# A deformable convolution, attention and mixture-of-experts kernel: the preparation of the next image held to a steady pace, and two products issued in 512 columns

## The chip, the cores and the metric

The kernel runs on one core of a Trainium2 chip. The time is the device time of one execution in microseconds. The kernel before took 7870.18 us (median of 3 runs, 7869.32 to 7878.19). The engines named below are PE (TensorE, matrix products), ACT (ScalarE, exponentials), DVE (VectorE), POOL (GpSimd, which here issues the gathers), SP (SyncE, which here issues nearly all other transfers) and the 16 DMA engines.

## The reference

The input is `x` of 4 images, 128 channels, 64 by 64 positions. Layer 0 adds to `x` a deformable 3x3 convolution of its group norm. Layer 1 takes the 4096 positions of an image as tokens of 128 channels: attention with 16 heads of 8 channels in which query, key and value are one and the same tensor, a small feed-forward part, and then 8 experts of which the two best are mixed for each token.

```python
# layer 0
x = x + deform_conv(group_norm(x), offsets and masks from two 3x3 convolutions)
# layer 1, per image: t is 4096 x 128
qkv = ring(cos(heads(ln(t)) + rx_theta))
scores = einsum("bhsd,bhtd->bhst", q, q) / sqrt(8)
ctx = einsum("bhst,bhtd->bhsd", softmax(scores), q)
t = t + ln(x1 + ffn(x1)),  x1 = ln(ln(t) + ctx @ w_comb.T)
t = t + sum over the top 2 of 8 experts of p_k * (ln(t) @ expert_w[k])
```

## The kernel before

**The attention loop.** For each image there are 4 groups of 4 heads, 8 chunks of 512 queries, and key tiles of 128. A *run* is one group and one chunk of queries over its key tiles; a *step* is one key tile of a run. There are 3700 steps, 964 in image 0 and 912 in each of the others. In a step PE makes scores for 4 heads (`scores`, L1155, four products into two PSUM tiles `sc` of 1024 columns), ACT takes their exponential (L1164, two instructions into SBUF tiles `e`), and PE multiplies them with the values (`context`, L1172, four products into `acc`). Scores are issued two steps ahead of the products that use them (`LAG = 2`, L1308); the `sc` tiles have 3 buffers, the `e` tiles 6.

**Turned tiles.** Scores are symmetric, so of two neighbouring chunks one block of 512 by 512 is computed once. `turn` (L1040) transposes the two `e` tiles of such a step on DVE into a tile with tag `st` (3 buffers), SP writes it to DRAM (`etd<-st`), and a later run reads it back (`et<-etd`) and uses it in `from_turned` (L1096, products at L1108).

**Work beside the loop.** Two kinds of work fill the rest of PE, DVE, POOL and the queues. `prepare(b)` makes the keys, queries and values of image b: group norm, a table of corners in DRAM, offsets, and then `deform` (L563), which goes through 96 *units* of three taps and 128 positions: a gather by POOL two units ahead (L575), three weighted sums on DVE (L589 to L592), three transposes into a tile that also has tag `st` (L599), and after each fourth unit a write to DRAM (`smd<-tr`, L612). Each of the 8 chunks of an image then goes through `convolved` (L633: read back as `sT`, L643, then the convolution as products of 256 columns) and `features` (L701). `finish(b, ch)` (L989) is the part behind attention: output projection, feed-forward and experts (L882, 16 products of 256 columns times four column blocks of 32).

**Who sets the order.** The order on PE, DVE, SP and POOL is fixed when the program is built, by the planner `Beside` (L62). It advances an estimated time by 1.82 us a step. Each piece of side work is a generator that yields `need(pe, dve, lat, hold)` before its next piece. In each step the planner takes at most one piece with PE work, and that only if it has credit: 0.44 us of PE a step are granted (`RATE`), at most 0.44 is saved up and 0.50 may be owed (`LATE`, L143); while the first image is streamed in, 1.0 us a step are granted. Among pieces that are ready the lowest rank goes first: turned products -1, `prepare` 0.5 or 2, `finish` 1 or 2. `prepare(b+1)` has rank 2 while its `progress` (L584) is ahead of `share`, the part of image b's steps that is done (counted to 80 steps before its end, L1333), and 0.5 while it is behind (L1334). Whatever of it is left at the last run of image b is drained (L1356). A piece with `hold=True` keeps the one PSUM bank for side work (`misc`) until its group is complete. The order on ACT, and which buffer of a pool a tile gets, is decided by the framework as the program is built.

**By columns.** `by_columns` (L270) makes a product of 128 output rows as four products of 32 rows, one on each column block of the array. An f32 product shows as two records in the profile, so one call shows as eight.

Of the kernel before, what the change touches and what calls it, by code (L numbers as in the profile page):

```python
# [22 lines left out]
P = 128  # L23
# [7 lines left out]
KK = 9  # L31
# [162 lines left out]
FREE = -1.0  # L194


def need(pe=0.0, dve=0.0, lat=0.0, hold=False, after=0.0):

    return pe, dve, lat, hold, after


def ve(n, ops=1):

    return ops * (0.17 + n / 960.0)


MM256 = 0.44
MM128 = 0.23  # L210

# [7 lines left out]
def kernel(  # L219
# [37 lines left out]
    prepared = {}  # L257

    progress = {}
    featuring = []  # L260


# [54 lines left out]
    wconv_sb = load(wconv, [P, KK, C], "wconv_sb")  # L317
# [245 lines left out]
    def deform(b, tab, idx, wt):  # L563


        AHEAD = NV - 1
        units = [
            (ch, kg, j) for ch in range(NCH) for kg in range(3) for j in range(4 * ch, 4 * ch + 4)
        ]

        def gather(_, kg, j):
            v = work.tile([P, 3, 4 * C], F32, tag="v", name=f"v{b}_{j}_{kg}", bufs=NV)
            for k in range(3):
                kk = 3 * kg + k
                nc.gpsimd.indirect_dma_start(  # L575
                    out=v[:, k, :], out_offset=None, in_=tab,
                    in_offset=bass.IndirectOffsetOnAxis(ap=idx[:, j, kk : kk + 1], axis=0),
                )
            return v, beside.gathered()

        sent = 0.0
        ahead = [gather(*units[n]) for n in range(AHEAD)]
        for n, (ch, kg, j) in enumerate(units):
            progress[b] = 0.1 + 0.9 * n / len(units)  # L584
            v, landed = ahead.pop(0)
            v4 = v.rearrange("p k (q c) -> p (k q) c", c=C)
            w12 = wt[:, j, 3 * kg : 3 * kg + 3, :].rearrange("p k q -> p (k q)")
            yield need(dve=ve(1536), after=landed)
            nc.vector.tensor_tensor(v4, v4, w12[:, :, None].to_broadcast([P, 12, C]), ALU.mult)  # L589
            yield need(dve=ve(768) + ve(384))  # L590
            nc.vector.tensor_tensor(v[:, :, : 2 * C], v[:, :, : 2 * C], v[:, :, 2 * C :], ALU.add)  # L591
            nc.vector.tensor_tensor(v[:, :, :C], v[:, :, :C], v[:, :, C : 2 * C], ALU.add)  # L592

            yield need(dve=ve(384))
            if j % 4 == 0:
                beside.flush(sent)
                tr9 = work.tile([P, 4, 4, 4, 32], F32, tag="st", name=f"tr{b}_{ch}_{kg}", bufs=NST)
            for k in range(3):
                nc.vector.transpose(  # L599
                    out=tr9[:, k, :, j % 4, :],  # L600
                    in_=v[:, k, :C].rearrange("p (c i) -> p c i", i=32),
                )
            if n + AHEAD < len(units):
                beside.later(beside.dve, lambda u=units[n + AHEAD]: ahead.append(gather(*u)))
            if j % 4 < 3:
                continue
            while kg == 0 and len(featuring) > 1:
                yield need(lat=1.0)

            def put(ch=ch, kg=kg, tr9=tr9):  # L610
                for o in range(4):
                    nc.sync.dma_start(  # L612
                        out=smd[ch % 2][:, 3 * kg : 3 * kg + 3, :, o].rearrange(
                            "i k c n -> i (k c) n"
                        ),
                        in_=tr9[32 * o : 32 * (o + 1), :3].rearrange("p k c j t -> p (k c) (j t)"),
                    )

            sent = beside.dve
            beside.later(sent, put)  # L620
            if kg == 2:

                while featuring:
                    yield need(lat=1.0)
                featuring.append(True)
                beside.later(
                    beside.dve + 0.1,
                    lambda ch=ch: beside.add("prepare", convolved(b, ch), 0.5, True),
                )
        while featuring:  # L630
            yield need(lat=1.0)

    def convolved(b, ch):  # L633

        xr = work.tile([P, CH], F32, tag="p2", name=f"xr{b}_{ch}", bufs=NP2)
        nc.sync.dma_start(out=xr, in_=xf[b, :, CH * ch : CH * (ch + 1)])
        yield need(lat=2.5)

        sT = big.tile([P, KK, CH], F32, tag="xs", name=f"sT{b}_{ch}")

        def get(kg):
            for c in range(4):
                nc.sync.dma_start(  # L643
                    out=sT[32 * c : 32 * (c + 1), 3 * kg : 3 * kg + 3],
                    in_=smd[ch % 2][:, 3 * kg : 3 * kg + 3, c].rearrange("i k o n -> i k (o n)"),
                )

        get(0)
        yield need(lat=6.0)
        get(1)  # L650
        yield need(lat=4.0)
        for k in range(KK):
            if k == 2:
                get(2)
            for hf in range(2):
                last = k == KK - 1 and hf == 1
                yield need(pe=MM256, dve=ve(128, 4) if last else 0.0, lat=0.2 if last else FREE, hold=not last)
                if k == 0 and hf == 0:
                    po = misc(f"conv_ps{b}_{ch}")
                by_columns(  # L660
                    po[:, 256 * hf : 256 * (hf + 1)], wconv_sb[:, k, :],
                    sT[:, k, 256 * hf : 256 * (hf + 1)], k == 0 and hf == 0, last,
                )
        for o in range(4):
            of_block = xr.rearrange("p (j o t) -> p j o t", o=4, t=32)[:, :, o]
            nc.vector.scalar_tensor_tensor(
                of_block, po[:, P * o : P * (o + 1)].rearrange("p (j t) -> p j t", t=32), bconv_sb,
                of_block, ALU.add, ALU.add,
            )
        yield need(pe=tr(4), dve=ve(512))  # L670
        pt = misc(f"x2_ps{b}_{ch}")
        for k in range(4):
            nc.tensor.transpose(pt[:, P * k : P * (k + 1)], xr[:, P * k : P * (k + 1)], ident)
        x2 = work.tile([P, 4, C], F32, tag="p2", name=f"x2_{b}_{ch}", bufs=NP2)
        nc.vector.tensor_copy(x2, pt.rearrange("p (i c) -> p i c", c=C))
        beside.later(beside.dve, lambda: nc.sync.dma_start(out=x2d[b][ch], in_=x2))
        mean = work.tile([P, 4], F32, tag="lt_m", name=f"mean{b}_{ch}")
        rstd = work.tile([P, 4], F32, tag="lt_r", name=f"rstd{b}_{ch}")
        yield from features(b, ch, x2, mean, rstd)
# [202 lines left out]
    def experts(b, ch, x4):  # L882
# [75 lines left out]
        for i in range(4):  # L958
            ws = [temp2(f"eo{b}_{ch}_{i}_{hf}") for hf in range(2)]
            for hf in range(2):  # L960
                for part in range(2):
                    yield need(pe=MM256, dve=ve(512) if part else 0.0, lat=FREE, hold=not part)
                    if part == 0:
                        pe = misc(f"e_ps{b}_{ch}_{i}_{hf}")
                    e0 = 4 * hf + 2 * part
                    by_columns(
                        pe[:, 256 * part : 256 * (part + 1)], uT[:, P * i : P * (i + 1)],
                        ew_sb[:, e0 : e0 + 2, :].rearrange("p e c -> p (e c)"), True, True,
                    )
                nc.vector.tensor_tensor(  # L970
                    ws[hf], pe.rearrange("p (e c) -> p e c", c=C),
                    gt[:, i, 4 * hf : 4 * (hf + 1), None].to_broadcast([P, 4, C]), ALU.mult,
                )
            yield need(dve=ve(512))
            w = ws[0]
            nc.vector.tensor_tensor(w, w, ws[1], ALU.add)
            yield need(dve=ve(256) + ve(128, 2), lat=0.2)
            nc.vector.tensor_tensor(w[:, :2, :], w[:, :2, :], w[:, 2:4, :], ALU.add)
            nc.vector.tensor_tensor(w[:, 0, :], w[:, 0, :], w[:, 1, :], ALU.add)
            nc.vector.tensor_tensor(x4[:, i, :], x4[:, i, :], w[:, 0, :], ALU.add)  # L980
# [319 lines left out]
    with tc.manual_schedule(engines={PE, DVE, SP, POOL}):  # L1300
# [6 lines left out]
        while n < len(steps):  # L1307
# [23 lines left out]
            if b + 1 < NB:  # L1331

                share = (n - begun) / (of_batch[b] - 80 - begun)  # L1333
                beside.rank("prepare", 2 if progress.get(b + 1, 0.0) > share else 0.5)  # L1334
            beside.step(backlog)
            if issued <= n + LAG and issued < len(steps) and at_hand(issued, n):
                continue
# [15 lines left out]
                beside.drain("turned")  # L1353
            if following:
                if following[0] != b and at == 0:
                    beside.drain("prepare")  # L1356

                if at == 1:
# [97 lines left out]
```

## Time and profile before

| what | us |
|---|---|
| median of 3 runs | 7870.18 |
| the profiled execution | 7908.98 |
| its span | 7907.1 |
| ACT busy, share of the span | 6874.6 (87%) |
| PE busy, share of the span | 7194.3 (91%) |
| DVE busy | 4487.9 (57%) |
| POOL busy | 1644.6 (21%) |
| mean granted TensorE clock | 0.954 |

The profiled execution took 7908.98 us, 0.5% more than the median. The span runs from the first to the last instruction. Times of records of PE overlap, since matmuls are pipelined: where the spacing of instructions matters it is read from their starts in the timeline. In the page, the line of a group gives its busy time, the mean of one, and the engine's idle time before it with what ended most of it. Image 0 is attended from 246 us on, image 1 from 2403 us, image 2 from 4249 us and image 3 from 6122 us; the last exponential of a step starts near 7821 us. POOL's slices show when `deform` runs.

### The profile page before, as it was taken

What the parts mean: (1) busy time and instruction counts of PE and PEld (TensorE: products, weight loads), DVE (VectorE), ACT (ScalarE), POOL (GpSimd) and SP (SyncE); (2) the same over time, 40 slices, a digit from 0 to 9 for tenths busy, and PEclk for the clock granted to TensorE, in tenths of its full rate; (3) what the DMA queues carried; (4) which work ended last, traced back from release to release, by engine and by line L of the source; (5) the groups of instructions that cost most, each with busy time, mean ns of one, the idle gap of its engine ahead of it and who ended that gap; (6) DMA issues with size and microseconds to landing.
All of it is one profiled execution on the core that took longest, in us unless ns stands there. A gap on an engine that the chain in (4) does not pass through costs nothing.

```text
span 7907.1 us, 182019 instructions
## 1 busy us (share of the span) xinstructions
PE 7194.3 (91%) x73664; PEld 2524.1 (32%) x73664; DVE 4487.9 (57%) x9024; ACT 6874.6 (87%) x7441; POOL 1644.6 (21%) x1326
## 2 busy tenths in 40 slices
PE   2378979999998999999999989989999999999997
PEld 1122222333333333333333333333333333333333
DVE  5666436666453667777554567766444554445434
ACT  0267978988998988989999988888999999999995
POOL 4544114343100332332000133432000000000000
PEclk6688988999999999999999999999999999999998
DMA  6776558888666878898666788988655577877762
GB/s 180 215 214 208 158 150 251 272 260 269 194 190 181 254 228 254 261 293 266 189 187 180 211 278 270 286 282 276 188 175 168 157 234 238 256 240 247 241 212 81
DMA packets 968439, 1757.98 MB, mean 222 GB/s; under 512 B 170864, under 2 KB 436088, under 8 KB 916908
## 3 DMA queue, kind: packets, MB, share of 16 engines
q1 hardware_dynamic: 862590, 1436.61, 60.1%
q0 software_dynamic: 92160, 302.06, 11.9%
q8 instruction: 578, 9.47, 0.5%
q10 hardware_dynamic: 12846, 7.67, 0.4%
q14 instruction: 265, 2.17, 0.1%
HBM read 1063.83 MB, written 682.13 MB: 221 GB/s over the span
## 4 chain that ended last, share of the span: by engine, by line
PE 78%; DMA 8%; DVE 3%; SPq 3%; issue 3%; ACT 3%; POOL 1%; another core or an unknown queue 0%; ACTq 0%; DVEq 0%; POOLq 0%
PE acc L1172 38%; PE sc L1155 23%; PE acc L1108 5%; PE e_ps L273 3%; PE conv_ps L273 3%; ACT e L1164 3%; PE f_ps L273 2%; DMA sT<-smd 2%; DMA et<-etd 1%; DMA kT<-kTd 1%; DMA etd<-st 1%; SPq L476 1%; PE om_ps L507 1%; DMA v<-tab,idx 1%; DVE v L589 1%
## 5 line engine op out<-in xcount | busy, mean ns | idle before, releaser
L1164 ACT ACTIVATE e<-sc 128x1024 f32<-128x1024 f32 x7400 | 6871.5, 1065 | 863.7 <-PE sc L1155 584.6
L1172 PE MATMUL acc<-e,qf 128*32 128x512 f32 x29600 | 3982.3, 608 | 46.1 <-DVE cu L1376 32.9
L1155 PE MATMUL sc<-qT,kT 32*128 32x512 f32 x14800 | 2404.0, 502 | 317.8 <-ACT e L1164 148.2
L1155 PEld LDWEIGHTS sc<-qT,kT 32*128 32x128 f32 x14800 | 960.2, 184 | 3745.1 <-ACT e L1164 3089.6
L575 POOL DMA_INDIRECT v<-tab,idx x1152 | 1444.7, 1254 | 1880.2 <-DVE tr L599 1158.3
L1046 DVE STREAM_TRANSPOSE st<-e 128x1024 f32<-128x1024 f32 x792 | 937.8, 1222 | 833.1 <-ACT e L1164 640.7
L1172 PEld LDWEIGHTS acc<-e,qf 128*32 128x32 f32 x29600 | 804.0, 110 | 614.4 <-issue 339.8
L375 POOL TENSOR_TENSOR r<-ln_t,expo 128x4 f32<-128x4 f32 x96 | 112.3, 1170 | 3151.2 <-DVE ln_t L373 3113.4
L589 DVE TENSOR_TENSOR v<-v,wt 128x1536 f32<-128x1536 f32 x384 | 665.9, 1734 | 103.6 <-DMA v<-tab,idx 78.5
L1108 PE MATMUL acc<-et,qf 128*32 128x128 f32 x12672 | 528.7, 283 | 55.5 <-DMA et<-etd 47.5
L273 PE MATMUL conv_ps<-sT,wconv_sb 128*32 128x256 f32 x4608 | 380.7, 407 | 125.0 <-DMA sT<-smd 121.9
L970 DVE TENSOR_TENSOR eo<-e_ps,gt 128x512 f32<-128x512 f32 x256 | 175.0, 685 | 548.7 <-PE e_ps L273 538.3
L1108 PEld LDWEIGHTS acc<-et,qf 128*32 128x32 f32 x12672 | 305.7, 110 | 259.3 <-issue 191.9
L591 DVE TENSOR_TENSOR v<-v 128x768 f32<-128x768 f32 x384 | 367.3, 957 | 10.7
L1374 DVE COPY cu<-acc 128x512 f32<-128x512 f32 x128 | 88.5, 691 | 442.0 <-PE acc L1172 392.6
L599 DVE STREAM_TRANSPOSE tr<-v 128x128 f32<-128x128 f32 x1152 | 266.0, 282 | 39.0 <-DMA etd<-st 21.1
L592 DVE TENSOR_TENSOR v<-v 128x384 f32<-128x384 f32 x384 | 215.4, 561 | 13.3
L273 PEld LDWEIGHTS conv_ps<-sT,wconv_sb 128*32 128x32 f32 x4608 | 96.9, 110 | 274.6 <-issue 255.1
L375 POOL TENSOR_TENSOR rstd<-lt_t,expo 128x4 f32<-128x4 f32 x32 | 54.3, 1696 | 554.8 <-DVE lt_t L373 554.8
L273 PE MATMUL f_ps<-w_sb,h 128*32 128x128 f32 x4096 | 165.4, 281 | 0.0
L855 DVE TENSOR_SCALAR h<-h_ps,b_sb 128x512 f32<-128x512 f32 x128 | 94.8, 743 | 102.3 <-PE h_ps L853 96.0
L1376 DVE TENSOR_TENSOR cu<-cu,acc 128x512 f32<-128x512 f32 x38 | 26.1, 686 | 207.1 <-PE acc L1172 118.9
(219 smaller groups left out, 3008.8 us busy)
## 6 DMA issues: line engine op xcount, KB each, us to landing
etd<-st SPq DMA_DIRECT2D x1584, 256.0 KB
et<-etd SPq DMA_DIRECT2D x396, 1024.0 KB
kT<-kTd SPq DMA_DIRECT2D x400, 256.0 KB
smd<-tr SPq DMA_DIRECT2D x384, 192.0 KB
sT<-smd SPq DMA_DIRECT2D x384, 192.0 KB
qf<-fqd SPq DMA_DIRECT2D x400, 144.0 KB
qT<-qTd SPq DMA_DIRECT2D x166, 256.0 KB
atd<-cu SPq DMA_DIRECT2D x128, 256.0 KB
```

The source lines that it names most:

```text
L273: nc.tensor.matmul(dst[c : c + 32], lhsT=lhsT[:, c : c + 32], rhs=rhs, start=start, stop=stop)
L575: nc.gpsimd.indirect_dma_start(out=v[:, k, :], out_offset=None, in_=tab, in_offset=bass.IndirectOffsetOnAxis(ap=idx[:, j, kk : kk + 1], ax ...
L589: nc.vector.tensor_tensor(v4, v4, w12[:, :, None].to_broadcast([P, 12, C]), ALU.mult)
L591: nc.vector.tensor_tensor(v[:, :, : 2 * C], v[:, :, : 2 * C], v[:, :, 2 * C :], ALU.add)
L592: nc.vector.tensor_tensor(v[:, :, :C], v[:, :, :C], v[:, :, C : 2 * C], ALU.add)
L599: nc.vector.transpose(out=tr9[:, k, :, j % 4, :], in_=v[:, k, :C].rearrange("p (c i) -> p c i", i=32),)
L970: nc.vector.tensor_tensor(ws[hf], pe.rearrange("p (e c) -> p e c", c=C), gt[:, i, 4 * hf : 4 * (hf + 1), None].to_broadcast([P, 4, C]), AL ...
L1046: nc.vector.transpose(out=st[:, :, 2 * pr : 2 * pr + 2, :].rearrange("p o h (q j) -> p o (h q) j", j=32), in_=es[pr].rearrange("p h (q o i ...
L1108: nc.tensor.matmul(acc[32 * h : 32 * (h + 1), P * kt : P * (kt + 1)], lhsT=qf[:, t, QW * h : QW * h + 32], rhs=e[:, :, h, 32 * t : 32 * (t ...
L1155: nc.tensor.matmul(ps[i // 2][:, i % 2, :], lhsT=kT[h : h + 32, P * (t % 4) : P * (t % 4 + 1)], rhs=qT[h : h + 32, :], start=True, stop=True,)
L1164: nc.scalar.activation(e, ps[pr], AF.Exp, scale=1.0 / math.sqrt(HD))
L1172: nc.tensor.matmul(acc[32 * h : 32 * (h + 1), :], lhsT=qf[:, t % 4, QW * h : QW * h + 32], rhs=es[h // 2][:, h % 2, :], start=(t == ts[0]) ...
```

## The change

1. **Pace.** A list `due` holds the present `share`. In `deform`, before each unit of images 1 to 3, the generator yields waits of 1.5 us while `progress` is more than 0.06 ahead of `due[0]`. At the last run of an image `due[0]` is set to 1.0 before the rest is drained.
2. **Convolution.** In `convolved` each tap is one piece of 512 columns (`MM512 = 0.86` us for the planner) instead of two of 256 (0.44 each): 9 pieces for a chunk, not 18.
3. **Experts.** In `experts` each half of the experts is one piece of 512 columns instead of two of 256: 8 pieces for a chunk, not 16. The evictions by DVE stay as they were.

```diff
+MM512 = 0.86
@@ tile_conv_attn_moe_kernel
+    due = [1.0]
@@ deform
             progress[b] = 0.1 + 0.9 * n / len(units)
+            while b and progress[b] > due[0] + 0.06:
+                yield need(lat=1.5)
@@ convolved
-            for hf in range(2):
-                last = k == KK - 1 and hf == 1
-                yield need(pe=MM256, dve=ve(128, 4) if last else 0.0, lat=0.2 if last else FREE, hold=not last)
-                if k == 0 and hf == 0:
-                    po = misc(f"conv_ps{b}_{ch}")
-                by_columns(
-                    po[:, 256 * hf : 256 * (hf + 1)], wconv_sb[:, k, :],
-                    sT[:, k, 256 * hf : 256 * (hf + 1)], k == 0 and hf == 0, last,
-                )
+            last = k == KK - 1
+            yield need(pe=MM512, dve=ve(128, 4) if last else 0.0, lat=0.2 if last else FREE, hold=not last)
+            if k == 0:
+                po = misc(f"conv_ps{b}_{ch}")
+            by_columns(po, wconv_sb[:, k, :], sT[:, k, :], k == 0, last)
@@ experts
-                for part in range(2):
-                    yield need(pe=MM256, dve=ve(512) if part else 0.0, lat=FREE, hold=not part)
-                    if part == 0:
-                        pe = misc(f"e_ps{b}_{ch}_{i}_{hf}")
-                    e0 = 4 * hf + 2 * part
-                    by_columns(
-                        pe[:, 256 * part : 256 * (part + 1)], uT[:, P * i : P * (i + 1)],
-                        ew_sb[:, e0 : e0 + 2, :].rearrange("p e c -> p (e c)"), True, True,
-                    )
+                yield need(pe=MM512, dve=ve(512), lat=FREE)
+                pe = misc(f"e_ps{b}_{ch}_{i}_{hf}")
+                by_columns(
+                    pe, uT[:, P * i : P * (i + 1)],
+                    ew_sb[:, 4 * hf : 4 * hf + 4, :].rearrange("p e c -> p (e c)"), True, True,
+                )
@@ the main loop
                 beside.rank("prepare", 2 if progress.get(b + 1, 0.0) > share else 0.5)
+                due[0] = share
@@ the main loop, at the last run of an image
                 if following[0] != b and at == 0:
+                    due[0] = 1.0
                     beside.drain("prepare")
```

## The prediction

> **What bounds the kernel now.** I read four views: the page, then stretches of the span (to find where time is lost), then the waits of PE and ACT, and the timeline of a bad and of a good stretch. The page's costliest groups:
>
> ```profile
> L1164 ACT ACTIVATE e<-sc 128x1024 f32<-128x1024 f32 x7400 | 6871.5, 1065 | 863.7 <-PE sc L1155 584.6
> L1172 PE MATMUL acc<-e,qf 128*32 128x512 f32 x29600 | 3982.3, 608 | 46.1 <-DVE cu L1376 32.9
> ```
>
> The stretches (time, then busy time and instructions of PE, PEld, DVE, ACT, POOL, the granted clock, the DMA share, GB/s):
>
> ```profile
> 1100.00:2000.00 900.00, 838.16 (x7468) 271.65 (x7460) 577.91 (x962) 789.67 (x850) 363.88 (x291) 0.96 0.83 258
> 2500.00:3800.00 1300.00, 1216.91 (x12805) 429.71 (x12805) 872.63 (x1670) 1156.05 (x1249) 390.18 (x313) 0.97 0.82 254
> 3800.00:4300.00 500.00, 499.45 (x5513) 179.58 (x5509) 253.65 (x572) 499.35 (x545) 14.35 (x15) 1.00 0.62 180
> 4400.00:5500.00 1100.00, 1006.89 (x9943) 346.78 (x9939) 772.64 (x1426) 939.09 (x1011) 387.19 (x309) 0.97 0.85 268
> 5500.00:6900.00 1400.00, 1398.36 (x15591) 505.11 (x15587) 686.28 (x1577) 1398.21 (x1525) 34.84 (x34) 1.00 0.68 204
> ```
>
> Where POOL is idle (no gathers, so no `deform`) ACT is never without work: 1525 exponentials in 1400 us, 1.089 a us. These stretches are bound by ACT, with PE just behind it. In the three stretches with gathers ACT stands still: at 1.089 a us they should hold 980, 1416 and 1198 exponentials and hold 850, 1249 and 1011, so 119, 153 and 172 us are lost. That is what can be won.
>
> How it is lost (timeline, PE and ACT):
>
> ```profile
> 4636.76 0.50 PE L1155 MATMUL sc<-qT,kT 32*128 32x512 f32 x2
> ...
> 4638.43 0.64 PE L273 MATMUL conv_ps<-sT,wconv_sb 128*32 128x256 f32 x8
> 4638.89 1.04 PE L1172 MATMUL acc<-e,qf 128*32 128x512 f32 x8
> 4639.86 0.50 PE L1155 MATMUL sc<-qT,kT 32*128 32x512 f32 x2
> 4641.10 0.50 PE L1155 MATMUL sc<-qT,kT 32*128 32x512 f32 x2 [0.74 <-ACT e L1164]
> ...
> 4640.02 1.94 ACT L1164 ACTIVATE e<-sc 128x1024 f32<-128x1024 f32 x2 [1.16 <-PE acc L1172]
> ```
>
> PE and ACT are in lockstep: the exponential waits for the context product, the next scores wait for the exponential, and a step takes 3.10 us (4636.76 to 4639.86, score to score) instead of 1.86. The reason is the `e` buffers. Counted in the built program by buffer address, most exponentials write where the one six before wrote; here they write where the one four before did, because a pair of buffers is held by a `turn` that DVE has not done. `turn` needs a tile `st`, and `deform` takes the same three for its transposes. The program before has 267 such writes at distance four: 79, 72 and 112 in steps 300 to 1000, 1000 to 1800 and 2000 to 2500, where `deform` runs, and 4 elsewhere. The waits of ACT and PE bear it out:
>
> ```profile
> ACT e L1164 <- PE acc L1172: 154.9, 135, 2.7
> ...
> PE conv_ps L273 <- DMA sT<-smd: 121.9, 6, 88.7
> PE sc L1155 <- DMA kT<-kTd: 81.6, 6, 27.1
> PE acc L1108 <- DMA et<-etd: 47.5, 14, 11.2
> ```
>
> The first is the lockstep. The others are single long waits for transfers, which DMA traffic (0.82 to 0.85 busy against 0.62 to 0.68) brings about.
>
> **The change, part by part.**
>
> *Pace.* It removes no instruction; 96 units an image remain with their gathers, transposes and transfers. It moves them. By the planner's own order the last unit of images 1, 2 and 3 stands at steps 763, 1604 and 2427 before and at 849, 1736 and 2649 after, counted from beginnings at 300, 975 and 1890. Units wait, so what hangs behind them, the convolution and features of their chunk, is later too, and `finish` takes the steps left free. At the last run all is drained as before, with no unit left.
>
> Lockstep: the changed program has 149 writes at distance four (42, 57, 34 in the same ranges, 16 elsewhere). A write cost 154.9 us / 267 = 0.58 us. 118 fewer save 68 us. Ends: 0, if DVE is late at other places than the program supposes, and -100, if the held pairs that remain are shorter too. I take 68, since the count is exact and the price an average over the same mechanism.
>
> Long waits: without the lockstep (0.58 x 79, 72, 112 = 46, 42, 65) the three stretches lose another 73, 111 and 107 us. The same work goes over 549 instead of 463 steps, 761 instead of 629, and 759 instead of 537. If the loss goes down as the density does, it falls by 16%, 17% and 29%, together 11 + 19 + 31 = 61 us. The two later stretches point that way: 629 steps lose 153 us in all, 537 steps lose 172. Ends: 0 and -61. I take -35, because waits for `et` and `kT` hang on the loop's own transfers too, which stay. SP is moved past nothing new: its transfers stay in their generators' order, and the wait of the pace is the planner's, not an engine's; no instruction stands behind it.
>
> *512 columns.* Records on PE fall by 2304 (convolution) and 2048 (experts); weight loads by as many; evictions stay. From starts in the timeline, a step with nothing beside takes PE 1.40 us, with a piece of 256 columns 1.86: such a piece costs 0.455. Context products of 512 columns that follow each other (24 records from 7821.16, the next start at 7823.73) take 0.86 each. So two pieces of 256 cost 0.91 and one of 512 costs 0.86. 1025 steps with a 256 piece become 527 with a 512 piece, and bare steps rise from 994 to 1493; 456 of the 527 are followed by a bare one. ACT needs 1.82 a step (its median in bare steps). Best end: 1025 steps of 1.865 all come down to 1.82, -46 us. Worst end: the long step takes 1.40 + 0.86 = 2.27, ACT starves and the bare step behind it makes up for nothing: 0.45 x 527 - 46 = +190. The nearest row is a transpose beside the loop:
>
> ```profile
> 6021.11 0.50 PE L1155 MATMUL sc<-qT,kT 32*128 32x512 f32 x4
> 6021.54 0.66 PE L795 MATMUL u_ps<-ident,u 128*128 128x128 f32 x4
> 6022.13 1.07 PE L1172 MATMUL acc<-e,qf 128*32 128x512 f32 x8
> 6023.12 0.51 PE L1155 MATMUL sc<-qT,kT 32*128 32x512 f32 x4
> 6023.56 1.07 PE L1172 MATMUL acc<-e,qf 128*32 128x512 f32 x8
> ```
>
> It costs PE 0.59, makes a step of 2.01, and the next takes 1.44 (scores at 6024.56): PE makes it up, and ACT's seven exponentials from 6018.90 run on nearly unbroken. A piece of 0.86 is 0.27 longer. If ACT had a full stock (two filled score tiles) it costs nothing, if it had none, up to 0.3. I take 0.1 x 527 - 46 = +5 us.
>
> The Trainium skill, "TensorE: Matmul & The Clock Gate", section "Back-to-back issue gap", gives a warm matmul N/2.4 + 2.5 ns, so that joining saves a constant of 2.5 ns a record. By it 4352 records fewer would be 11 us of PE, an estimate; by the rows here 544 joined pieces x 0.05 = 27 us. Either is PE time, which is not what ends a bare step.
>
> *Opening.* Up to step 300 the loop waits for each chunk's keys, and credit allows a piece every step. Nine pieces fewer stand in the chain of each of 8 chunks. Worth 0 if `sT` lands last anyway (121.9 us of waits say it often does), 8 x 9 x 0.45 = -32 if not. I take -10.
>
> *The end.* Behind the last step stand the experts of one chunk as before; in the last 50 steps and after, the planner issues 26.4 us of estimated side work against 27.9. 0 us.
>
> Sum: -68 - 35 + 5 - 10 = -108 us. The profiled execution of 7909 us would come to 7801; against the median of 7870, 7762. I say 7765.
>
> **Rivals.**
> - *R1, the long pieces starve ACT (slower).* PE works in order, so scores stand behind 0.86 us. For: in chains of 1.86 us steps PE has no lead left, and 31 of the 527 steps are followed by another. Against: the credit puts a bare step behind most. At 0.35 us a piece: 527 x 0.35 - 46 = +138, with the gains of the pace 7870 + 138 - 113 = 7895. It decides from 0.3 us a piece on.
> - *R2, the pace does not help: the change doesn't do what it says.* Waits stay with each unit, however far apart, and `deform` now lies beside more of `finish`, whose transfers share the queue. For: stretch 2500:3800 already had `finish` beside it and lost 153 us. With half of the lockstep's gain, no other: 7870 - 34 + 5 = 7841; with none 7875.
> - *R3, more than forecast.* Both ends of the pace and the best of the columns: -100 - 61 - 25 = 7684.
>
> **How the numbers follow.** Forecast (7710 to 7815) 0.50; R1 0.12; R2 (7815 to 7880) 0.20; R3 (below 7710) 0.18. 0.2% is 16 us, about what a measurement can tell from no change. Faster than 7854: 0.50 + 0.18 + seven tenths of R2 = 0.82; within: 0.06; slower: 0.12. The range of 8 in 10 is 7675 to 7885: it leaves out most of R1 and the far part of R3.
>
> **What would show it.** POOL's slices busy evenly over images 1 and 2 up to about 150 us before their end, DMA share there at most 0.80; ACT's wait for `acc` L1172 near 87 us (from 154.9); in 4400:5500 more than 1090 exponentials (from 1011); records at `conv_ps` and `e_ps` of 512 columns with half the count; in 6900:7700, where only experts change, ACT's busy share still 98% or more. If that last falls below 95%, R1 is right. If `acc` waits fall and the time does not, another wait took over, most likely `et` or `sT`.

## The result: no change that can be measured

| | before | after |
|---|---|---|
| median of 12 runs each | 7872.39 | 7869.26 |
| lowest and highest | 7859.82 to 7882.81 | 7848.26 to 7888.01 |
| the profiled execution | 7908.98 | 7848.26 |

The ratio of after to before is 0.9997, with a 95% interval of 0.9985 to 1.001. The forecast was 7765 us. The two profiles are 61 us apart, far more than the medians: that of before was taken in an execution some 37 us above its median, that of after in one 21 us below. A difference read from these two profiles is therefore too good by up to 58 us, and what follows leans on runs made side by side on one chip.

The page's two large groups after the change (`e` is now written at L1162, the context product stands at L1170):

```profile
L1162 ACT ACTIVATE e<-sc 128x1024 f32<-128x1024 f32 x7400 | 6893.8, 1067 | 779.7 <-PE sc L1153 566.9
L1170 PE MATMUL acc<-e,qf 128*32 128x512 f32 x29600 | 3994.0, 608 | 31.5 <-DVE cu L1376 20.3
```

ACT's idle time ahead of its exponentials fell from 863.7 to 779.7 us, but the part put down to scores hardly did (584.6 to 566.9). The same stretches as before, with the same columns, and the last one that the prediction named:

```profile
1100.00:2000.00 900.00, 850.76 (x7132) 265.17 (x7128) 555.11 (x927) 809.58 (x871) 347.75 (x276) 0.97 0.83 256
2500.00:3800.00 1300.00, 1244.63 (x12018) 419.81 (x12014) 852.93 (x1665) 1181.41 (x1274) 333.35 (x288) 0.99 0.78 243
3800.00:4300.00 500.00, 483.20 (x4939) 168.78 (x4931) 263.80 (x566) 470.83 (x511) 32.22 (x30) 0.99 0.71 208
4400.00:5500.00 1100.00, 1040.09 (x9901) 347.72 (x9903) 723.90 (x1410) 984.43 (x1060) 282.02 (x246) 0.98 0.81 250
5500.00:6900.00 1400.00, 1387.30 (x14257) 480.51 (x14249) 749.92 (x1650) 1359.74 (x1473) 101.71 (x85) 1.00 0.72 219
6900.00:7700.00 800.00, 794.15 (x8691) 286.00 (x8687) 383.11 (x911) 781.67 (x851) 20.16 (x20) 1.00 0.72 227
```

The three stretches with gathers hold more exponentials than before (871, 1274 and 1060 for 850, 1249 and 1011: 95 more). The two that were without a gap hold fewer: 511 for 545, and 1473 for 1525, 86 less, although PE's clock is nearly full in them (some of the gathers now reach into the last one: 101.71 us of POOL instead of 34.84). In these two profiles what is won in the one kind of stretch is given back in the other. The waits say what kind of gap it is; the first line is from the kernel before, the others are from after:

```profile
ACT e L1164 <- PE sc L1155: 584.6, 196, 159.9
```

```profile
ACT e L1162 <- PE sc L1153: 566.9, 568, 154.0
...
ACT e L1162 <- PE acc L1170: 95.7, 83, 3.7
PE conv_ps L276 <- DMA sT<-smd: 94.9, 4, 86.8
ACT e L1162 <- remote: 70.2, 30, 5.1
PE sc L1153 <- DMA kT<-kTd: 63.0, 3, 26.2
...
PE acc L1106 <- DMA et<-etd: 48.0, 9, 11.6
```

The wait for `acc`, the lockstep, fell from 154.9 to 95.7 us. The wait for scores has its sum as before but comes 568 times instead of 196: many short ones have come. The timeline of a stretch without gathers shows them, PE first, then ACT. In what follows, a *long piece* is a piece of 512 columns, a *bare step* one with no side work on PE, and the *stock* is what filled score tiles hold for ACT:

```profile
6427.99 0.75 PE L1153 MATMUL sc<-qT,kT 32*128 32x512 f32 x4
6428.67 1.06 PE L276 MATMUL e_ps<-ew_sb,u_4T 128*32 128x512 f32 x8
6429.55 1.04 PE L1170 MATMUL acc<-e,qf 128*32 128x512 f32 x8
6430.52 0.51 PE L1153 MATMUL sc<-qT,kT 32*128 32x512 f32 x4
6430.96 1.06 PE L1170 MATMUL acc<-e,qf 128*32 128x512 f32 x8
6431.95 0.75 PE L1153 MATMUL sc<-qT,kT 32*128 32x512 f32 x4
```

```profile
6427.16 3.77 ACT L1162 ACTIVATE e<-sc 128x1024 f32<-128x1024 f32 x4 [0.18 <-PE sc L1153]
6431.12 3.77 ACT L1162 ACTIVATE e<-sc 128x1024 f32<-128x1024 f32 x4 [0.20 <-PE sc L1153]
6435.09 3.77 ACT L1162 ACTIVATE e<-sc 128x1024 f32<-128x1024 f32 x4 [0.19 <-PE sc L1153]
```

A long piece and the bare step behind it take 3.96 us (6427.99 to 6431.95). Four exponentials take 3.77 and then ACT is dry for 0.18 to 0.20 us, each time. PE's own work would fit: the scores at 6430.52 take 0.44 us to the next start, but those at 6427.99, behind the bare step, take 0.68. There PE is early; its first two score products go at once, and the other two start at 6428.23, 0.05 us after the exponential begun at 6427.16 has ended: they wait for a score tile that ACT still reads. Then 0.88 us of long piece and 0.97 of context product stand ahead of the next scores. In that time ACT uses up what three score tiles can hold: it ends its fourth exponential near 6430.93 and has the next scores at 6431.12. The full stock at the start of the long piece lasts 2.26 us (6428.67 to 6430.93), and the way to the next exponential takes 2.45. PE loses time behind the bare step because there is no room, and lacks it in front of the next scores. Over all such pairs between 5600 and 7600 us the median from context product to context product is 3.957 us for `e_ps` (99 pairs) and 3.951 for `conv_ps` (16); before, two steps with pieces of 256 took 3.730 (176 pairs). That is 0.23 us for each long piece. Two such steps in the kernel before, during which ACT runs without a break:

```profile
5677.09 0.51 PE L1155 MATMUL sc<-qT,kT 32*128 32x512 f32 x4
5677.52 0.64 PE L273 MATMUL e_ps<-ew_sb,u_5T 128*32 128x256 f32 x8
5677.98 1.04 PE L1172 MATMUL acc<-e,qf 128*32 128x512 f32 x8
5678.95 0.51 PE L1155 MATMUL sc<-qT,kT 32*128 32x512 f32 x4
5679.39 0.64 PE L273 MATMUL e_ps<-ew_sb,u_5T 128*32 128x256 f32 x8
5679.84 1.04 PE L1172 MATMUL acc<-e,qf 128*32 128x512 f32 x8
5680.81 0.51 PE L1155 MATMUL sc<-qT,kT 32*128 32x512 f32 x4
```

### The profile page after: what moved, and what is told of

It reads as the page before. It is cut to its first block, busy times and chain, and to the rows that moved or that the text cites. A ratio compares the mean times of both kernels' runs of the same rounds, so it can differ in the third digit from the quotient of the medians.

```text
span 7846.3 us, 173269 instructions
## 1 busy us (share of the span) xinstructions
PE 7248.3 (92%) x69312; PEld 2439.6 (31%) x69312; DVE 4486.9 (57%) x9024; ACT 6897.0 (88%) x7441; POOL 1589.5 (20%) x1326
## 3 DMA queue, kind: packets, MB, share of 16 engines
q14 instruction: 264, 2.16, 0.1%
## 4 chain that ended last, share of the span: by engine, by line
PE 82%; DMA 6%; DVE 3%; issue 3%; ACT 2%; SPq 2%; POOL 1%; another core or an unknown queue 0%; ACTq 0%; POOLq 0%; DVEq 0%
PE acc L1170 40%; PE sc L1153 25%; PE acc L1106 5%; PE conv_ps L276 3%; PE e_ps L276 3%; PE f_ps L276 2%; ACT e L1162 2%; DMA et<-etd 1%; DMA sT<-smd 1%; POOL v L578 1%; PE om_ps L510 1%; DMA v<-tab,idx 1%; DVE v L594 0%; DMA qT<-qTd 0%; PE ao_ps L276 0%
## 5 line engine op out<-in xcount | busy, mean ns | idle before, releaser
L1162 ACT ACTIVATE e<-sc 128x1024 f32<-128x1024 f32 x7400 | 6893.8, 1067 | 779.7 <-PE sc L1153 566.9
L1170 PE MATMUL acc<-e,qf 128*32 128x512 f32 x29600 | 3994.0, 608 | 31.5 <-DVE cu L1376 20.3
L1153 PE MATMUL sc<-qT,kT 32*128 32x512 f32 x14800 | 2481.7, 500 | 236.2 <-ACT e L1162 101.9
L1153 PEld LDWEIGHTS sc<-qT,kT 32*128 32x128 f32 x14800 | 1024.5, 183 | 3666.3 <-ACT e L1162 2758.6
L578 POOL DMA_INDIRECT v<-tab,idx x1152 | 1383.3, 1201 | 2098.0 <-DVE tr L604 1381.2
L1170 PEld LDWEIGHTS acc<-e,qf 128*32 128x32 f32 x29600 | 755.6, 110 | 868.8 <-issue 769.6
L276 PE MATMUL conv_ps<-sT,wconv_sb 128*32 128x512 f32 x2304 | 315.3, 623 | 103.3 <-DMA sT<-smd 94.9
L732 POOL COPY fx<-rn 128x512 f32<-128x512 f32 x32 | 32.1, 1003 | 632.7 <-DVE rn L731 540.0
```

Source lines behind the costliest of these rows:

```text
L276: nc.tensor.matmul(dst[c : c + 32], lhsT=lhsT[:, c : c + 32], rhs=rhs, start=start, stop=stop)
L578: nc.gpsimd.indirect_dma_start(out=v[:, k, :], out_offset=None, in_=tab, in_offset=bass.IndirectOffsetOnAxis(ap=idx[:, j, kk : kk + 1], ax ...
L1153: nc.tensor.matmul(ps[i // 2][:, i % 2, :], lhsT=kT[h : h + 32, P * (t % 4) : P * (t % 4 + 1)], rhs=qT[h : h + 32, :], start=True, stop=True,)
L1162: nc.scalar.activation(e, ps[pr], AF.Exp, scale=1.0 / math.sqrt(HD))
L1170: nc.tensor.matmul(acc[32 * h : 32 * (h + 1), :], lhsT=qf[:, t % 4, QW * h : QW * h + 32], rhs=es[h // 2][:, h % 2, :], start=(t == ts[0]) ...
```

## The experiments

The theory formed from this (A): each long piece outside the opening costs 0.23 us, and that eats what the pace wins. Its first rival (B): the pieces are free and the pace did not win. The kernels came in three groups, each beside the kernel before on one chip, on which that kernel took 7736.26 us (e1 to e5), 7886.76 (e6 to e9) and 7740.48 (e10 to e13). The chips differ by 2%, so times are compared within a group.

**Pace alone (e1, and again e11).** `convolved` and `experts` as before the change (the edit is shortened):

```diff
-            yield need(pe=MM512, ...)
-            by_columns(po, wconv_sb[:, k, :], sT[:, k, :], k == 0, last)
+            for hf in range(2):
+                yield need(pe=MM256, ...)
+                by_columns(po[:, 256 * hf : 256 * (hf + 1)], wconv_sb[:, k, :],
+                    sT[:, k, 256 * hf : 256 * (hf + 1)], k == 0 and hf == 0, last)
...  (experts likewise, in two parts of 256)
```

> The pace alone; convolution and experts stay in pieces of 256 columns. Theory A (the pace wins as forecast, the long pieces lose as much): in the changed kernel a long step and the bare step behind it take 3.96 us, two steps with 256 columns each 3.73, so 0.23 us a piece; without the 463 long pieces outside the opening the time falls by about 105 us from 7870 to 7765, ACT's wait for acc below 100 us, and the stretch 5500 to 6900 us has 1510 or more exponentials. Theory B (the pace wins nothing in total, the lost time only moves into the later part of an image): 7855 to 7885.

Measured: 7677.82 us, ratio 0.9921 (0.9909 to 0.9933): 58 us faster. The pair of steps with pieces of 256 is back at 3.730 us. B falls. A expected 105 us; the 58 are short of that because this kernel ends differently: from the start of the last step's exponentials to the end of the span it takes 142 us, against 86 in before and 81 in after, so the loop itself is some 115 us shorter. ACT's wait for `acc` is 101.0 us (expected: below 100), and 5500 to 6900 us holds 1507 exponentials (expected: 1510 or more). With the pace and without long pieces, one more chunk's experts stand behind the last step; that the planner's granted PE time gets through less of `finish` in the loop is the likely reason, read from its rules and not tested. The timeline of ACT at the end (of e11, the same kernel), and the same of before:

```profile
7524.71 7.45 ACT L1168 ACTIVATE e<-sc 128x1024 f32<-128x1024 f32 x8
7562.51 0.23 ACT L926 ACTIVATE ex<-lg 128x32 f32<-128x32 f32 x1 [30.36 <-DVE lg L925]
7631.01 0.23 ACT L926 ACTIVATE ex<-lg 128x32 f32<-128x32 f32 x1 [68.27 <-DVE lg L925]
```

```profile
7814.50 8.40 ACT L1164 ACTIVATE e<-sc 128x1024 f32<-128x1024 f32 x9
7879.25 0.23 ACT L922 ACTIVATE ex<-lg 128x32 f32<-128x32 f32 x1 [56.34 <-DVE lg L921]
```

Each `ex` is the gate of one chunk's experts: two behind the last step with the pace alone, one before.

**512 columns alone (e2).** The change without the wait in `deform`; `due` is still set, but nothing reads it:

```diff
-            while b and progress[b] > due[0] + 0.06:
-                yield need(lat=1.5)
```

> The products of 512 columns alone, without the pace. Theory A: 463 pieces outside the opening at 0.23 us are +106 us, the opening's shorter chains give some 50 us back, fewer writes at distance four some 20: 7905, slower than before. Theory B: pieces of 512 columns cost nothing, 7870 or less.

Measured: 7874.77 us, ratio 1.0188 (1.0172 to 1.0204): 139 us slower. B falls, and A, which expected 35 us, is 104 us short. The pair is 3.958 us as in after. 464 long pieces lie outside the opening and ahead of the last step (9 x 8 x 3 of the convolution, 64 x 4 of the experts less 8); 464 x 0.23 = 107 us. The opening wins 22 to 40 (below), so some 54 to 72 us are left over. This kernel waits longer for transfers than the changed one on a chip of nearly the same speed (e10): 142.9 us in 15 waits for `sT` against 107.5 in 7, and 99.6 in 21 for `et` against 57.1 in 11. Together 78 us, which would be enough. ACT's waits point the same way: behind the first 600 exponentials, its waits for scores of 0.1 to 0.6 us come to 87 us in both kernels (418 and 426 waits), while those over 3 us come to 188 us in 24 waits, against 90 in 13 in e10. That the long pieces and the bunched gathers cause these long waits together is argued, not shown.

**Length or width (e4).** The changed kernel, each long piece made of two products of 256 columns one behind the other:

```diff
-            by_columns(po, wconv_sb[:, k, :], sT[:, k, :], k == 0, last)
+            for hf in range(2):
+                by_columns(po[:, 256 * hf : 256 * (hf + 1)], wconv_sb[:, k, :],
+                    sT[:, k, 256 * hf : 256 * (hf + 1)], k == 0 and hf == 0, last and hf == 1)
...  (experts likewise)
```

> The changed kernel, but each long piece holds two products of 256 columns instead of one of 512; planning and order are the same. Theory A (the length of the piece between two sets of scores matters): the same loss, 0.05 us of PE more a piece, 7870 to 7895, and the pair of a long and a bare step takes 3.96 us or a little more. Rival (the width of 512 columns itself matters, by its writes or its weight loads): the pair goes back to 3.73 us and the time to about 7765.

Measured: 7702.41 us, ratio 0.9951 (0.9937 to 0.9965). The timeline of PE:

```profile
6289.17 0.75 PE L1159 MATMUL sc<-qT,kT 32*128 32x512 f32 x4
6289.85 1.07 PE L276 MATMUL e_ps<-ew_sb,u_4T 128*32 128x256 f32 x16
6290.73 1.04 PE L1176 MATMUL acc<-e,qf 128*32 128x512 f32 x8
6291.71 0.51 PE L1159 MATMUL sc<-qT,kT 32*128 32x512 f32 x4
6292.15 1.06 PE L1176 MATMUL acc<-e,qf 128*32 128x512 f32 x8
6293.14 0.73 PE L1159 MATMUL sc<-qT,kT 32*128 32x512 f32 x4
```

Sixteen records of 256 columns stand where eight of 512 stood, and the next start comes 0.88 us later as before; the pair takes 3.97 us (6289.17 to 6293.14; median 3.965). So it is how long PE is away from the scores that counts, not the width of a product. The time lies between the two forecasts, because their common start of 7870 us did not hold on this chip. The saving of 2.5 ns a record, which the prediction worked out from the Trainium skill ("TensorE: Matmul & The Clock Gate", section "Back-to-back issue gap"), can't be told here. That section gives its formula as the gap of a matmul by itself and says that it is off in a stream of weight loads and matmuls. The kernel with the 4352 records more has a ratio of 0.9951, the changed one 0.9942 on another chip (0.9928 to 0.9955, e10); the difference is some 7 us, and with intervals over 20 us wide neither 0 nor the 11 us estimated from the section is ruled out.

**The convolution in 512 columns for image 0 only, and the pace (e5, and again e12).**

```diff
+            if b == 0:
+                yield need(pe=0.86, ...)
+                by_columns(po, wconv_sb[:, k, :], sT[:, k, :], k == 0, last)
+                continue
             for hf in range(2):
...
```

> The pace, 512 columns for the convolution of image 0 alone, 256 everywhere else. Theory A with the opening's gain real (steps 0 to 300 took 49 us less in the changed kernel's profile): 7765 - 45 = 7720. Rival (the opening's difference is one between executions): the same as the pace alone.

Measured: 7637.41 us, ratio 0.9879 (0.986 to 0.9897): 40 us faster than the pace alone. In the first image, where steps wait for keys, the long piece wins.

**The changed kernel once more (e6), and with experts in 256 columns (e7),** on the slower chip.

> The changed kernel itself, beside the others. Its first comparison gave a ratio of 0.9997 with the kernel before at 7872; the comparison of the first four experiments had the kernel before at 7736. If the balance of gain and loss hangs on how long transfers take on a chip, the ratio here is that of the twin with two products of 256 a piece (0.995) less up to 0.003 for PE: 0.992 to 0.995. If not: 0.9997 again, and then the width of 512 columns costs 0.005 more than two of 256.

> The changed kernel with the experts back in pieces of 256 columns: pace and wide convolution. Theory A (0.23 us a long piece outside the opening, here 215 of them, 49 us; against the kernel with the wide convolution in the opening alone, ratio 0.988): 0.988 + 0.006 = 0.994, if the last experts end as late as there. Rival (only the experts' long pieces cost, the convolution's lie in stretches that wait anyway): 0.988 or less.

Measured: e6 7909.57 us, ratio 1.003 (1.0015 to 1.0044); e7 7884.2, ratio 0.9985 (0.997 to 1.0). The wide experts thus cost 25 us, although they shorten the end from 126 to 80 us; in the loop they cost 71, which is 0.29 for each of 248 pieces. (By the ratios the cost is 35 us, and 0.33 a piece.) The ratio of e7 is above both its forecasts, 0.994 and 0.988. That e6 is slower than before was not expected by either theory; see the last section.

**A version that keeps what wins (e8):** pace, wide convolution for image 0, wide experts for images 2 and 3, so that `finish` keeps up with the end.

```diff
+                if b >= NB - 2:
+                    yield need(pe=0.86, dve=ve(512), lat=FREE)
...
+                else:
+                    for part in range(2):
...
```

> Pace, wide convolution in the opening, and wide experts for images 2 and 3 alone, meant to take back the 61 us by which the pace with narrow experts ends later behind its last step (142 us against 81). 128 long pieces at 0.23 us cost 29; the planner's own count of side work behind the last step falls to that of the changed kernel. Theory A: 0.988 + 0.004 - 0.007 = 0.985. Rival (the end is late for another reason): 0.991.

Measured: 7837.37 us, ratio 0.9928 (0.9907 to 0.995), 72 us faster than the changed kernel beside it. 90 us lie behind the start of the last step's exponentials, so the end was won back, but the ratio is above both forecasts (0.985 and 0.991), which came from the faster chip. On a fast chip the same kernel has 0.9848 (e13).

**The price of the lockstep (e9).** The kernel before with `NST = 2` instead of 3, so that `turn` and `deform` share two tiles. It has 746 writes of exponentials at distance four instead of 267.

```diff
-NST = 3
+NST = 2
```

> The kernel before with two st tiles instead of three, nothing else. Writes of exponentials at distance four go from 267 to 746. Theory A (the lockstep is bound to these held pairs, 0.58 us a write): +278 us at most, and at least half of it, since some of the steps wait for transfers anyway; ACT's wait for acc above 300 us. Rival (the pairs only stand for another wait of DVE): within 30 us of the kernel before.

Measured: 8170.11 us, ratio 1.0351 (1.0322 to 1.038), 277 to 283 us more for 479 more writes: 0.58 to 0.59 us each. The rival falls, and the prediction's 0.58 holds. (With two tiles `deform` waits for them as well; this run can't tell its part apart.) The wait:

```profile
ACT e L1164 <- PE acc L1172: 466.3, 366, 9.1
```

It is 311 us above the 154.9 of before, 0.65 us a write. The opposite, `NST = 4`, wasn't run.

**All four side by side (e10 to e13),** five rounds on one chip, with kernels known from above (after, e1, e5, e8):

> The changed kernel beside the three others on one chip. Theory A (each long piece outside the opening costs 0.23 us): against pace alone (e11) it loses 455 pieces x 0.23 = 105 us, wins 40 us in the opening and 60 us behind the last step, so it stands 5 us above e11, between 10 below and 30 above. Rival B (the pieces cost nothing, and the earlier difference was one of chips): 100 us below e11. Exponentials' waits for scores near 600 us, for acc near 96 us.

> Pace alone. Both theories: faster than the kernel before by 20 to 60 us (ratio 0.992 to 0.997), with exponentials' waits for acc near 100 us and some 140 us from the last exponential to the end.

> Pace, and the convolution in 512 columns for image 0 only. Theory A: 40 us below e11 (e5 against e1), between 20 and 50, and so some 45 us below e10. Rival B: 40 us below e11 and 60 us above e10.

> As e12, with the experts of images 2 and 3 in 512 columns. Theory A: 111 pieces x 0.23 = 26 us lost against e12 and 52 us won behind the last step, so 26 us below e12, between 0 and 50 below. Rival B: 52 us or more below e12. If the end is made up for elsewhere (Theory C): 26 us above e12.

| kernel | us | ratio to before | 95% | last step's exponentials to the end |
|---|---|---|---|---|
| before | 7740.48 | | | (86) |
| e10, the change | 7696.54 | 0.9942 | 0.9928 to 0.9955 | 80 |
| e11, pace alone | 7674.69 | 0.9917 | 0.9904 to 0.9931 | 143 |
| e12, and wide opening | 7652.62 | 0.9884 | 0.9868 to 0.99 | 142 |
| e13, and wide experts at the end | 7616.22 | 0.9848 | 0.9835 to 0.9861 | 90 |

(The 86 us of before are from its profile on the first chip.) The changed kernel stands 22 us above the pace alone; A expected 5, between 10 below and 30 above, B 100 below. Against e12, which differs from it only in long pieces outside the opening, it loses 44 us and wins 62 behind the last step, so its loop costs 106 us more: 0.23 for each of the 464 pieces. The price from whole runs is not the same everywhere: e13 against e12 wins 36 us in all and 52 behind the last step, so 120 long pieces cost it 16 us, 0.13 each, and e7 gave 0.29. The waits for scores of e10, and then of e11, agree with the cause:

```profile
ACT e L1162 <- PE sc L1153: 539.5, 510, 155.4
ACT e L1162 <- PE acc L1170: 95.8, 84, 7.4
```

```profile
ACT e L1168 <- PE sc L1159: 469.0, 75, 159.2
...
ACT e L1168 <- PE acc L1176: 98.5, 97, 2.6
```

510 waits against 75, while the lockstep is the same. (The forecast for e10 was near 600 us for scores; it is 539.5.) e13 is the fastest, 1.5% below before and 1.0% below the changed kernel.

## Why the prediction was wrong, point by point

- *Lockstep, -68.* Right in mechanism and nearly in size: the wait fell by 59 us (154.9 to 95.7; forecast near 87), and e9 gives the price again. Nearly all of it is the pace: the wait is 101.0 and 98.5 us with the pace alone (e1, e11) and 143.0 with the wide pieces alone (e2).
- *Long waits, -35.* Where it can be told apart, the pace won more. Pace alone is 58 and 66 us faster and has some 57 us more behind its last step, so its loop is some 115 to 123 us shorter, against 68 + 35 = 103 forecast. The wait for `acc` can be compared across chips, for the changed kernel has 95.7, 96.4 and 95.8 us of it on three. It falls by 54 (e1) and 56 us (e11), so 61 and 67 us are other waits, at or above the 61 that the prediction set as the far end. Which of them fell, these runs don't separate, for the kernel before has no trace on a fast chip.
- *512 columns, +5.* This step failed. Of its two parts the -46 was to come from steps that PE ends; the +0.1 us a piece was taken from the transposes beside the loop (a step of 2.01, then one of 1.44, in all 3.45). The measured price is 0.23 us a piece net, +107 us. In the prediction's own terms, which set the -46 apart and give ACT 1.82 us a step, it is 3.957 - 3.64 = 0.32 a piece, against the 0.1 that it took. The transpose was the wrong row: its piece is 0.59 us long and stands alone, with stock on both sides. With 0.59 in place of 0.88 the way to the next exponential would take 2.16 us (an estimate from the timeline above), less than the 2.26 that the stock lasts. The long pieces come every other step, 0.88 us long, so the stock must be rebuilt in one bare step, and it can't be: three score tiles hold too little. The prediction's condition, "If ACT had a full stock (two filled score tiles) it costs nothing", is what the timeline refutes. Behind nearly every bare step the stock is full and PE stands still because of it (of 90 such sets of scores ahead of a long piece of the experts, between 5600 and 7600 us, 87 take over 0.60 us to the next start instead of 0.44), and ACT still runs dry at the end of the next long piece.
- *Opening, -10.* Too small: 22 us (e12 against e11) to 40 (e5 against e1); the bound was 32.
- *The end, 0.* Right for the change (86 to 81 us). It hid a term: the pace by itself loses 57 us there, and the wide pieces win it back.
- *The sum.* With the measured terms, -119 + 107 - 22 (or 40) - 5 = -39 to -57 us. Side by side the change won 44 us on one chip (e10), which fits. On the chip of the record it won 3, and on a third it lost 23 (e6). The long pieces explain the step from the forecast to these -39 to -57 us; the 36 to 54 us that are missing on the chip of the record are no term of the prediction, and their cause stays open (see the last section).
- *Rivals.* R1 named the mechanism, and its price of 0.35 us a piece was near: in the same terms 0.32 was measured, just above the 0.3 from which it was to decide. That the change is not slower on the chip of the record is due to the pace and the opening, which won more than forecast. R2's range holds the measured time, but for the wrong reason where the chips are fast: the pace helps there. On the slower chips the pace was not run alone, so how far R2 is true there stays open.
- *What would show it.* POOL's slices came out more even. DMA's share is 0.83, 0.78 and 0.81, not all below 0.80. 4400:5500 holds 1060 exponentials, not 1090. ACT's share in 6900:7700 is 97.7%: the bound of 95% for R1 was too coarse, since 0.19 us in 3.96 is 5% even where long pieces follow each other without a pause.

## What to carry to other kernels

A queue worked off in order has a price for the length of a piece apart from its total: where the consumer lives on a few buffers, ask how long it can run on what they hold, and compare that with the longest stretch in which the producer is away. A step of spare time behind a long piece is worth only what the buffers can store of it. And look at how the last unit of work ends: a change that makes the side work slower or faster is paid behind the last step, where nothing hides it.

## What the runs showed of the hardware that was not expected

- Two score products alone take PE as long as four. In the lockstep of before, the pair at 4641.10 is followed by the convolution at 4641.53, 0.43 us later, and four in one go take 0.43 too (6021.11 to 6021.54). Over the whole trace the median is 0.43 us for two behind a wait (232 times) and 0.44 for four in one go. A score step that is cut in two by a wait is therefore longer by the whole delay of its second pair: the 0.68 us above are 0.25 to the start of the second pair and 0.43 from there on.
- The chip matters as much as the change. The kernel before took 7736 and 7740 us on two chips, 7872 and 7887 in the other two comparisons. The variants keep their distances (e8 is 72 us below e6, e13 80 below e10), but against before all of them stand worse on the slower chip: after 0.9942 and 1.003, the best version 0.9848 and 0.9928. In the traces of the slower ones ACT has waits which belong to no engine or queue that the program uses ("remote": 55.9 us in 26 waits before, 70.2 in 30 after, 113.7 in 46 in e8), all of them within 3 us of a gather that POOL issues; the eight profiles of the two faster chips have none. More waits of this kind are put down to scores. I counted the exponentials behind the first 600 that wait over 0.1 us though their scores ended over 0.26 us earlier, and whose wait is put down to scores, "remote" or "issue" (the lockstep is not among them). These waits come to 147 us before, 153 after, 185 in e6 and 214 in e8, and to 2 us or less in the profiles of the faster chips. Of the 117 of before 115 begin within 3 us of the start of a gather, and 129 of 131, 146 of 149 and 144 of 146 in the others, where 27 to 29% of all exponentials do. They are about what the slower chips cost: between profiles of the same kernel the span differs by 134 us (after and e10), 213 (e6 and e10) and 225 (e8 and e13), these waits by 153, 184 and 212. So part of what the first profiles put down to scores (86 of 584.6 us before, 90 of 566.9 after) is no lack of scores. What stops ACT there, and why the paced kernels lose more by it, stays open: no run here tells it.
